# Attention of a macaron block: maxima split out of PSUM, keys projected on four column strips, numerators of two heads in one PSUM bank

## The chip, the cores and the metric

The kernel runs on one core of a Trainium2 chip. The metric is the device time of one execution in microseconds, lower is better. A core has five engines that run their own instruction streams in order: TensorE (PE in the profile, its weight loads PEld), VectorE (DVE), ScalarE (ACT), GpSimd (POOL) and SyncE (SP), which issues most transfers; 16 DMA engines move the data.

## The reference

The input x is 16 sequences (batches) of 512 tokens with 128 features, float32. Six steps follow each other, each added to x:

```python
x = x + 0.5 * _L0_ffn_ref(_layernorm(x), ...)   # small per-channel network ("kan")
x = x + _L0_attn_ref(_layernorm(x), ...)        # causal attention
x = x + 0.5 * _L0_ffn_ref(_layernorm(x), ...)
x = x + 0.5 * _L1_ffn_ref(_layernorm(x), ...)   # 8 experts choose 128 tokens each
x = x + _L1_attn_ref(_layernorm(x), ...)        # linear recurrence over tokens
x = x + 0.5 * _L1_ffn_ref(_layernorm(x), ...)
```

The change lies in the causal attention. It has 16 query heads of 8 features in 4 groups; the 4 heads of a group share one key and one value head. Queries and keys are turned by rotary cosines and sines:

```python
q = (x @ Wq) ...; k = (x @ Wk) ...; v = (x @ Wv) ...
q = q * cos + rotate_half(q) * sin
k = k * cos + rotate_half(k) * sin
att = softmax(where(causal, q @ k.T * HD ** -0.5, lowest))
y = (att @ v) @ Wo
```

## The kernel before

Sizes: P = 128 partitions, S = 512 tokens in NT = 4 chunks of 128, HD = 8, NR = 4 groups of NG = 4 heads.

**Queries and keys** (`attn_in`, L414 to L485). After the norm, xT holds a batch transposed, features on partitions. Queries are projected to [128, 512] (`ps_pa`, and with swapped halves `ps_pb`), keys and their swapped form in one matmul to [64, 512] (`ps_pk`, L435), values to `ps_v` (L443). DVE multiplies them by cosines and sines out of PSUM, POOL adds (L439, L462). `parts` (L392) splits a float32 value into three bfloat16 parts: a cast on ACT and three subtractions on POOL. `spread` writes the parts to DRAM (`qs`, `ks`), and transfers bring them back into the packed tiles: a group's `qp[r]` has 72 rows, every pair of query part and key part by 8 features; `kp` has the matching rows. So one bfloat16 matmul over 72 rows gives a score of float32 precision. Rows 96 to 98 of `qp` get the negated row maximum in three parts, against rows of ones in `kp`.

**Maxima** (`maxima`, L596). For batch b+1, scores with queries on partitions go to `ps_sc`, one tile per entry of `BANKS` (11 per group), and DVE reduces each to row maxima (L615, L620) in `maxs`, 32 columns per half of the heads. `max_rows` (L624) splits them into three bfloat16 parts with four operations on [128, 32], transposes each chunk on PE (`ps_m`, L641), copies the result to `mr` [24, 512] and sends it over DRAM (`ms`) into rows 96 to 98 of two `qp` tiles.

**Weights and numerators** (`weights`, L656; `outputs`, L684). For batch b, scores with keys on partitions and the maximum already subtracted go to `ps_st`; ACT takes the exponential into `pt`, POOL clears what lies above the diagonal (L678). Per group, 16 matmuls (`ps_av`, L696) multiply by the values `va`, 32 columns wide per head: 8 values, a column of ones (the denominator), the rest zeros. The 4 heads of a group lie on the four strips of 32 partitions of one bank. ACT copies the bank to `oT`, PE transposes it (`ps_oq`, L709), DVE divides (L713, L714) into `y`. `stage_out` multiplies by Wo and goes on.

**Order.** The order of PE, ACT, DVE and POOL is written out by hand by generators. A loop over batches (L1144) has 44 turns, one score tile of `weights` and one of `maxima` each; the other stages (`kan`, `attn_in`, `outputs`, `gated`) are generators in `urgent` and `sides` that emit a piece per turn. `need` and `take` (L220, L226) give each turn a budget per engine, `bank` hands out two PSUM banks (tag `mm`), `later` holds work for the start of the next turn. `taken` counts groups whose weights are emitted; `attn_in` waits on it before it overwrites a `qp` tile. Before the loop there is a fill (b = -1, `filling`): the first batches' `kan` and `attn_in`, and the maxima of batch 0 alone. After the loop the experts run (`experts`, L896), with the recurrence between their two rounds.

**Queues.** SP issues nearly all transfers in program order: loads, `qs`, `ks`, `kp`, `qp`, `ms`. ACT's queue issues eight small loads at the start.

## Time and profile before

| | us |
|---|---|
| three runs | 1643.77, 1643.75, 1638.86 |
| median | 1643.75 |
| profiled execution | 1642.42 |
| its span | 1640.6 |
| PE busy in the span | 1542.4 (94%) |
| DVE, ACT, POOL busy | 1134.6, 1007.3, 1020.0 |
| share of PE in the chain that ended last | 70%; DVE 18% |

The span runs from the first to the last instruction. Matmuls are pipelined, so busy PE is not PE at its peak, and a row's mean duration is longer than what one more matmul adds. A row such as `L709 PE MATMUL ps_oq<-ident,oT 128*128 128x128 f32 x256 | 39.4, 276 | 0.5` reads: source line, engine, operation, result from operands, shape, count; busy us and mean ns; idle time of the engine just before, and what ended it. The chain is followed back from the last instruction, at each step to what released it or to the instruction before it on its engine.

### The profile page before, as it was taken

The numbers are of one execution on the slowest core, as the hardware profiler recorded it, in microseconds if no ns is written. First come the engines' busy times: TensorE is split into PE (matmuls) and PEld (weight loads), VectorE is DVE, ScalarE is ACT, GpSimd is POOL, SyncE is SP. The second block draws the span as 40 slices with busy tenths as digits, with TensorE's granted clock in tenths as the row PEclk, the third lists the DMA queues.
The fourth block names the chain that finished last, engine by engine and source line by source line (L and its number), as shares of the span: only waits on it lengthen the run. The fifth ranks groups of instructions, "written<-read, shape, count | busy, mean of one in ns | idle before, by whom it ended". The sixth has DMA issues, their size and how long they took to land.

```text
span 1640.6 us, 35158 instructions
## 1 busy us (share of the span) xinstructions
PE 1542.4 (94%) x12813; PEld 1074.8 (66%) x12813; DVE 1134.6 (69%) x3616; ACT 1007.3 (61%) x2016; POOL 1020.0 (62%) x1486
## 2 busy tenths in 40 slices
PE   5689999999999999999998899999999999999998
PEld 2234444444445444445454479999998899999998
DVE  6577878888888888888988334875569654762322
ACT  3336667877778777777766866444453444545444
POOL 2634555566655664565553666767766677777774
PEclk9779989999999999999999999999999999999999
DMA  5210110111111100110122213333332333333333
GB/s 128 66 66 24 54 50 28 41 57 50 31 43 52 56 26 36 57 43 29 45 71 62 58 41 62 69 66 73 69 73 56 72 62 78 70 71 73 74 73 57
DMA packets 103252, 94.91 MB, mean 58 GB/s; under 512 B 13229, under 2 KB 91638, under 8 KB 102838
## 3 DMA queue, kind: packets, MB, share of 16 engines
q1 hardware_dynamic: 76220, 67.72, 13.3%
q0 software_dynamic: 26048, 24.93, 9.0%
q8 instruction: 101, 1.65, 0.4%
q14 instruction: 73, 0.60, 0.1%
q10 hardware_dynamic: 810, 0.02, 0.0%
HBM read 59.07 MB, written 37.49 MB: 59 GB/s over the span
## 4 chain that ended last, share of the span: by engine, by line
PE 70%; DVE 18%; ACT 4%; issue 3%; POOL 3%; DMA 1%; SPq 0%; ACTq 0%; DVEq 0%; POOLq 0%
PE ps_h L939 12%; PE ps_y L954 12%; PE ps_av L696 7%; PE ps_st L673 6%; PE ps_sc L610 6%; DVE below L615 5%; PE acc L972 5%; PE ps_kg L364 4%; PE ps_s L337 3%; PE ps_t L317 3%; ACT pt L676 2%; DVE ln_st L286 2%; DVE tok L797 2%; PE ps_ko L385 2%; PE ps_g L749 1%
## 5 line engine op out<-in xcount | busy, mean ns | idle before, releaser
L678 POOL TENSOR_SCALAR_AFFINE_SELECT pt<-pt 128x128 f32<-128x128 f32 (+2 forms) x704 | 250.8, 363 | 333.3 <-ACT pt L676 328.5
L676 ACT ACTIVATE pt<-ps_st 128x512 f32<-128x512 f32 x682 | 368.2, 563 | 96.8 <-PE ps_st L673 91.0
L615 DVE CUSTOM_DVE_ANT_0 below<-ps_sc,causal 128x512 bf16<-128x512 f32 (+1 forms) x512 | 315.1, 615 | 79.9 <-PE ps_sc L610 64.4
L864 POOL DMA_INDIRECT xg<-xnd,tokI x256 | 250.6, 979 | 77.0 <-issue 39.5
L941 ACT ACTIVATE mo<-ps_h 128x512 f32<-128x512 f32 x256 | 152.6, 596 | 232.9 <-PE ps_h L939 232.5
L939 PE MATMUL ps_h<-xin,mw 128*128 128x128 f32 x2048 | 277.6, 278 | 0.0
L954 PE MATMUL ps_y<-mw,mo 128*128 128x128 f32 x2048 | 271.1, 275 | 2.2 <-DVE mo L963 2.2
L610 PE MATMUL ps_sc<-kp,qp 72*128 72x512 bf16 (+3 forms) x1024 | 261.3, 307 | 11.4 <-DVE maxs L615 6.9
L673 PE MATMUL ps_st<-qp,kp 99*128 99x512 bf16 x992 | 251.9, 305 | 16.7 <-ACT pt L676 16.1
L939 PEld LDWEIGHTS ps_h<-xin,mw 128*128 128x128 f32 x2048 | 249.7, 192 | 5.5 <-issue 3.4
L954 PEld LDWEIGHTS ps_y<-mw,mo 128*128 128x128 f32 x2048 | 249.2, 192 | 3.3 <-DVE mo L963 3.1
L986 POOL DMA_INDIRECT sum<-ye,tokI x124 | 201.6, 1626 | 67.5 <-issue 31.8
L673 PEld LDWEIGHTS <-kp 99*128 99x128 bf16 x1024 | 95.2, 101 | 177.8 <-issue 159.9
L370 ACT ACTIVATE kan_h<-kan_s,rbias,kw 128x512 f32<-128x512 f32 x256 | 205.7, 812 | 3.5 <-PE ps_kg L364 3.5
L696 PE MATMUL ps_av<-pt,va 128*32 128x512 f32 (+3 forms) x2048 | 164.4, 439 | 0.0
L620 DVE TENSOR_REDUCE maxs<-ps_sc 128x2 f32<-128x512 f32 (+1 forms) x192 | 130.1, 685 | 39.1 <-PE ps_sc L610 38.7
L610 PEld LDWEIGHTS <-qp 72*128 72x128 bf16 x1024 | 97.1, 100 | 80.1 <-issue 57.5
L960 DVE TENSOR_TENSOR mo<-mo 128x128 bf16<-128x128 f32 x132 | 38.2, 289 | 129.4 <-ACT mo L945 129.2
L972 PE MATMUL acc<-mo 128*128 128x128 bf16 x1584 | 111.4, 219 | 3.9 <-DVE mo L960 3.8
L696 PEld LDWEIGHTS ps_av<-pt,va 128*32 128x32 f32 x2048 | 53.5, 109 | 93.6 <-issue 43.0
L972 PEld LDWEIGHTS <-mo 128*128 128x128 bf16 x1584 | 99.4, 98 | 18.8 <-issue 17.6
L293 POOL TENSOR_TENSOR ln_rstd<-ln_rstd,mhalf 128x4 f32<-128x4 f32 x96 | 100.5, 1047 | 8.0
(194 smaller groups left out, 2340.5 us busy)
## 6 DMA issues: line engine op xcount, KB each, us to landing
qp<-qs SPq DMA_DIRECT2D x64, 288.0 KB
xnd<-kan_x SPq DMA_DIRECT2D x32, 256.0 KB
sum<-x SPq DMA_DIRECT2D x31, 256.0 KB
qs<-qpart SPq DMA_DIRECT2D x48, 128.0 KB
kp<-ks SPq DMA_DIRECT2D x48, 96.0 KB
x<-in_L_attn_x_dram SPq DMA_DIRECT2D x16, 256.0 KB
mw<-in_L_ffn_w_dram SPq DMA_DIRECT2D x16, 256.0 KB
xg<-xnd,tokI POOLq DMA_INDIRECT x256
```

The costliest lines, as they stand in the source:

```text
L370: nc.scalar.activation(h, sk[half], AF.Relu, bias=rbias[:, half, v : v + 1], scale=kw1[:, half, v : v + 1])
L610: nc.tensor.matmul(v[:, u, 0:n], lhsT=qp[r][0 : 9 * HD, g, bass.ts(c, P)], rhs=kp[0 : 9 * HD, r, 0:n], start=alone, stop=(u == len(gs) - 1 ...
L615: nc.vector.tensor_tensor_reduce(below[:, 0:n], v[:, 0, 0:n], causal[:, S - n : S], 1.0, LOWEST, ALU.add, ALU.max, accum_out=maxs[:, c, h ...
L673: nc.tensor.matmul(v[:, u, 0:n], lhsT=kp[ROWS, r, bass.ts(c, P)], rhs=qp[r][ROWS, g, c * P : S], start=True, stop=True)
L676: nc.scalar.activation(o, v[:, :, 0:n], AF.Exp, scale=HD ** -0.5)
L678: nc.gpsimd.affine_select(out=dg, in_=dg, compare_op=ALU.is_ge, fill=0.0, base=0, pattern=[[0, len(gs)], [1, P]], channel_multiplier=-1)
L696: nc.tensor.matmul(po[32 * g : 32 * g + 32, c * P : S], lhsT=va[:, c, r, :], rhs=pt[:, g, OFF[c] : OFF[c] + n], start=(c == 0), stop=(c == ...
L864: nc.gpsimd.indirect_dma_start(out=xgs[i // E % 2][:, i % E, :], out_offset=None, in_=xnd[b], in_offset=bass.IndirectOffsetOnAxis(ap=tokI[ ...
L939: nc.tensor.matmul(pst[:, f, :], lhsT=mw1[e][:, bass.ts(f, P)], rhs=xins[i // E % 2][:, i % E, :], start=True, stop=True)
L954: nc.tensor.matmul(py, lhsT=hs[u][:, f, :], rhs=mw2[e][:, f, :], start=(f == 0), stop=(f == NF - 1))
L972: nc.tensor.matmul(acc[:, c, :], lhsT=sels[u][:, bass.ts(c, P)], rhs=yes[u][:, w, :], start=(e == 0 and c == 0 and w == 0), stop=(e == las ...
L986: nc.gpsimd.indirect_dma_start(out=sums[k, b], out_offset=bass.IndirectOffsetOnAxis(ap=tokI[g][:, n : n + 1], axis=0), in_=ye[:, b % 2 * ( ...
```

## The change

- **Keys.** Keys are projected chunk by chunk: 8 matmuls of 128 columns put each chunk of 128 tokens on its own strip of 32 partitions, so that the keys are [128, 128] instead of [32, 512], plain and swapped side by side in one bank, the values behind them in the same bank. One product with a new table `ropek` (8 small loads on ACT's queue) replaces two; the addition, cast and subtractions run on 128 columns. The feature order of `wk` is changed.
- **Packed rows.** The rows of `qp` and `kp` stand in another order: in `qp` the three copies of a row are neighbours, in `kp` the three parts. Each `kp` transfer reads all three parts; a wait on `taken` stands before them.
- **Maxima.** They are written into one of two fixed tiles `topped` [128, 128], cleared once; one float32 transpose puts 32 of its columns on partitions, and four operations split them there, reading PSUM. `ms` is written in runs of 128 tokens, in the fill from ACT's queue.
- **Numerators.** Of two groups, the second's values stand 16 columns further in `va`, and both accumulate into one bank; copy, transposes and division happen once for two groups. The rows of `wo` are loaded in the matching order, in 8 transfers behind the loads of x.
- `parts` takes POOL's budget as an argument, 0.5 for keys; `stage_out` waits two turns more in the loop.

```diff
...
         nc.scalar.dma_start(out=gate_sb, in_=gate_in)
+        KR = NR * HD
+        ropek = cst.tile([P, 2, P], F32, name="ropek")
+        for j in range(NT):
+            for w in range(2):
+                src = rope_in[0:HD, w, bass.ts(j, P)].unsqueeze(1).to_broadcast([HD, NR, P])
+                nc.scalar.dma_start(out=ropek[j * KR : (j + 1) * KR, w, :], in_=src)
         rbias = cst.tile([P, 2, NV], F32, name="rbias")
...
         w2d = cst.tile([P, 2, NV, MH], F32, name="w2d")
+        topped = [cst.tile([P, P], F32, name=f"topped{i}") for i in range(2)]
+        for i in range(2):
+            nc.gpsimd.memset(topped[i], 0.0)
         eye4 = cst.tile([P, MH], F32, name="eye4")
...
-        KR = NR * HD
         wq = cst.tile([D, NH, HD], F32, name="wq")
         nc.sync.dma_start(out=wq, in_=wq_in.rearrange("k (h d) -> k h d", d=HD))
-        wk = cst.tile([D, 2, NR, HD], F32, name="wk")
-        nc.sync.dma_start(out=wk[:, 0, :, :], in_=wk_in.rearrange("k (h d) -> k h d", d=HD))
+        wk = cst.tile([D, 2, HD, NR], F32, name="wk")
+        nc.sync.dma_start(out=wk[:, 0, :, :].rearrange("k d h -> k (d h)"), in_=wk_in)
         wv = cst.tile([D, KR], F32, name="wv")
...
         wo = cst.tile([D, D], F32, name="wo")
-        nc.sync.dma_start(out=wo, in_=wo_in)
         rope = cst.tile([P, 2, S], F32, name="rope")
...
             load(b)
+        for i in range(NR // 2):
+            for g in range(NG):
+                src = wo_in[i * M : (i + 1) * M, :].rearrange("(j g d) n -> g j d n", j=2, g=NG)[g]
+                nc.sync.dma_start(out=wo[i * M + g * 2 * HD : i * M + (g + 1) * 2 * HD, :], in_=src)
         hh = HD // 2
...
+        def spread_keys(part, name):
+
+            scr = tc.dram_tile([3, HD, NR, S], BF16, name=name)
+            for i in range(3):
+                nc.sync.dma_start(out=scr[i].rearrange("d r (j t) -> j (d r) t", j=NT), in_=part[:, i, :])
+            return scr
+
         def attn_in(b, st):
             _, xT = yield from norm(x[b])
-            ka = w1p.tile([KR, S], F32, name="rope_ka")
-            kb = w1p.tile([KR, S], F32, name="rope_kb")
+            ka = w1p.tile([P, 2, P], F32, name="rope_ka")
             ta = w1p.tile([P, S], F32, name="rope_a")
...
             qpart = w1p.tile([P, 3, S], BF16, name="qpart")
-            kpart = w1p.tile([KR, 3, S], BF16, name="kpart")
+            kpart = w1p.tile([P, 3, P], BF16, name="kpart")
             pa = yield from bank([P, S], F32, "ps_pa", 0.9)
...
             freed()
-            pk = yield from bank([2 * KR, S], F32, "ps_pk", 0.9)
-            nc.tensor.matmul(pk, lhsT=wk.rearrange("k w h d -> k (w h d)"), rhs=xT, start=True, stop=True)
-            later.append(lambda: nc.vector.tensor_mul(ka, pk[0:KR, :], rope[0:KR, 0, :]))
+            pkv = yield from bank([P, 3, P], F32, "ps_kv", 1.3)
+            for w in range(2):
+                for j in range(NT):
+                    nc.tensor.matmul(pkv[j * KR : (j + 1) * KR, w, :], lhsT=wk[:, w, :, :].rearrange("k d h -> k (d h)"),
+                                     rhs=xT[:, bass.ts(j, P)], start=True, stop=True)
+            pv = pkv[:, 2, :].rearrange("p (c n) -> p c n", n=KR)
+            for c in range(NT):
+                nc.tensor.matmul(pv[:, c, :], lhsT=xT[:, bass.ts(c, P)], rhs=wv, start=True, stop=True)
+            later.append(lambda: nc.vector.tensor_mul(ka, pkv[:, 0:2, :], ropek))
             yield
...
             nc.gpsimd.tensor_tensor(ta, ta, tb, ALU.add)
-            take(dve=0.7)
-            pv = yield from bank([P, NT, KR], F32, "ps_v", 0.9)
-            for c in range(NT):
-                nc.tensor.matmul(pv[:, c, :], lhsT=xT[:, bass.ts(c, P)], rhs=wv, start=True, stop=True)
-            later.append(lambda: nc.vector.tensor_mul(kb, pk[KR : 2 * KR, :], rope[KR : 2 * KR, 1, :]))
-            yield
-            take(dve=0.7)
-            freed()
-            qp_steps = parts(ta, qpart, nc.scalar.copy, act=0.6)
+            take(dve=0.4)
+            qp_steps = parts(ta, qpart, nc.scalar.copy, 1.15, act=0.6)
             step(qp_steps)
...
             va = vap.tile([P, NT, NR, 32], F32, name="va")
-            nc.gpsimd.memset(va[:, :, :, HD:32], 0.0)
-            nc.gpsimd.memset(va[:, :, :, HD : HD + 1], 1.0)
-            later.append(lambda: nc.vector.tensor_copy(va[:, :, :, 0:HD], pv.rearrange("p c (r d) -> p c r d", d=HD)))
-            yield
-            take(dve=0.3)
+            nc.gpsimd.memset(va, 0.0)
+            mine = [va[:, :, j::2, 2 * HD * j : 2 * HD * (j + 1)] for j in range(2)]
+            for to in mine:
+                nc.gpsimd.memset(to[:, :, :, HD : HD + 1], 1.0)
+
+            def values():
+                from_ = pv.rearrange("p c (r j d) -> p c r j d", j=2, d=HD)
+                for j, to in enumerate(mine):
+                    nc.vector.tensor_copy(to[:, :, :, 0:HD], from_[:, :, :, j, :])
+
+            later.append(values)
+            yield
+            take(dve=0.4)
             freed()
...
             def keys():
-                yield from need(pool=1.25)
-                nc.gpsimd.tensor_tensor(ka, ka, kb, ALU.add)
-                yield
-                yield
-                yield
-                yield from parts(ka, kpart, nc.scalar.copy, act=0.6)
+                yield from need(pool=0.5)
+                keys_ = ka[:, 0, :]
+                nc.gpsimd.tensor_tensor(keys_, keys_, ka[:, 1, :], ALU.add)
+                yield
+                yield
+                yield from parts(keys_, kpart, nc.scalar.copy, 0.5, act=0.3)
...
-            ks = spread(kpart, NR, f"ks{b}")
+            ks = spread_keys(kpart, f"ks{b}")
             qs = spread(qpart, NH, f"qs{b}")
             N = 3 * HD
-            for j in range(3):
-                nc.sync.dma_start(
-                    out=kp[j * N : (j + 1) * N, :, :],
-                    in_=ks[j].rearrange("d r t -> d (r t)").unsqueeze(0).to_broadcast([3, HD, NR * S]),
-                )
+            while taken[0] < NR * (b - NKP + 1):
+                yield
+            for i in range(3):
+                nc.sync.dma_start(out=kp[i * N : (i + 1) * N, :, :],
+                                  in_=ks.rearrange("j d r t -> d j (r t)"))
             for r in range(NR):
...
                 nc.sync.dma_start(out=qp[r][0 : 3 * N, :, :],
-                                  in_=src.unsqueeze(0).to_broadcast([3, N, NG * S]))
-            yield
-
-        def centered(ps, w):
+                                  in_=src.unsqueeze(1).to_broadcast([N, 3, NG * S]))
+            yield
+
+        def centered(ps, w, to=None):
...
             nc.tensor.matmul(ps, lhsT=center, rhs=w, start=True, stop=True)
-            nc.vector.tensor_copy(w, ps)
+            if to is None:
+                nc.vector.tensor_copy(w, ps)
+            else:
+                nc.vector.tensor_copy(to, ps.rearrange("k (h d) -> k d h", d=HD))
...
             for half in range(2):
-                maxs = w2p.tile([P, NT, NH // 2], F32, name="maxs")
+                maxs = topped[half][:, 0 : NT * NH // 2].rearrange("p (h c) -> p h c", c=NT)
                 for r in (2 * half, 2 * half + 1):
...
                                 below[:, 0:n], v[:, 0, 0:n], causal[:, S - n : S], 1.0, LOWEST,
-                                ALU.add, ALU.max, accum_out=maxs[:, c, h : h + 1],
+                                ALU.add, ALU.max, accum_out=maxs[:, h, c : c + 1],
                             )
                         else:
-                            nc.vector.tensor_reduce(maxs[:, c, h : h + len(gs)], v[:, :, 0:n], AX.X, ALU.max)
+                            nc.vector.tensor_reduce(maxs[:, h : h + len(gs), c], v[:, :, 0:n], AX.X, ALU.max)
                         yield
-                urgent.append(max_rows(b, half, maxs))
-
-        def max_rows(b, half, maxs):
+                urgent.append(max_rows(b, half))
+
+        def max_rows(b, half):
             H2 = NH // 2
+            N = NT * H2
+            yield
+            pm = yield from bank([P, P], F32, "ps_m", 0.2)
+            nc.tensor.transpose(pm, topped[half], ident)
+            r = pm[0:N, :]
+            mr = w1p.tile([N, 3, P], BF16, name="mr")
+
+            def first():
+                nc.vector.tensor_scalar_mul(mr[:, 0, :], r, -1.0)
+                nc.vector.scalar_tensor_tensor(mr[:, 1, :], in0=r, scalar=-1.0, in1=mr[:, 0, :],
+                                               op0=ALU.mult, op1=ALU.subtract)
+
+            later.append(first)
+            yield
+            take(dve=0.45)
             yield from need(dve=0.45)
-            ms = w2p.tile([P, NT, 3, H2], BF16, name="ms")
-            r = w2p.tile([P, NT, H2], F32, name="ms_r")
-            nc.vector.tensor_scalar_mul(ms[:, :, 0, :], maxs, -1.0)
-            nc.vector.scalar_tensor_tensor(r, in0=maxs, scalar=-1.0, in1=ms[:, :, 0, :],
-                                           op0=ALU.mult, op1=ALU.subtract)
-            yield
-            yield from need(dve=0.45)
-            nc.vector.tensor_copy(ms[:, :, 1, :], r)
-            nc.vector.tensor_sub(ms[:, :, 2, :], r, ms[:, :, 1, :])
-            yield
-            yield
-            pm = yield from bank([3 * H2, NT, P], BF16, "ps_m", 0.3)
-            for c in range(NT):
-                nc.tensor.transpose(pm[:, c, :], ms[:, c, :, :].rearrange("p i h -> p (i h)"), identb)
-            mr = w1p.tile([3 * H2, S], BF16, name="mr")
-            later.append(lambda: nc.vector.tensor_copy(mr, pm.rearrange("p c q -> p (c q)")))
-            yield
-            take(dve=0.4)
-            freed()
+            nc.vector.scalar_tensor_tensor(r, in0=r, scalar=-1.0, in1=mr[:, 0, :], op0=ALU.mult, op1=ALU.subtract)
+            nc.vector.tensor_sub(mr[:, 2, :], r, mr[:, 1, :])
+            freed()
+            yield
             scr = tc.dram_tile([3, H2, S], BF16, name=f"ms{b}_{half}")
-            nc.sync.dma_start(out=scr.rearrange("i h t -> (i h) t"), in_=mr)
+            queue = nc.scalar if filling[0] else nc.sync
+            queue.dma_start(out=scr.rearrange("i h (c t) -> (h c) i t", c=NT), in_=mr)
             for k in range(2):
-                nc.sync.dma_start(out=packed(b)[0][2 * half + k][MXR : MXR + 3, :, :],
+                queue.dma_start(out=packed(b)[0][2 * half + k][MXR : MXR + 3, :, :],
                                   in_=scr[:, k * NG : (k + 1) * NG, :])
...
             pt, va, y = st["pt"].pop(r), st["va"], st["y"]
-            yield
-            po = avp.tile([P, S], F32, name="ps_av")
+            pair, odd = r // 2, r % 2
+            yield
+            if not odd:
+                st["po"] = avp.tile([P, S], F32, name="ps_av")
+            po = st["po"]
             for c in range(NT):
...
                     nc.tensor.matmul(po[32 * g : 32 * g + 32, c * P : S], lhsT=va[:, c, r, :],
-                                     rhs=pt[:, g, OFF[c] : OFF[c] + n], start=(c == 0), stop=(c == NT - 1))
+                                     rhs=pt[:, g, OFF[c] : OFF[c] + n], start=(c == 0 and not odd),
+                                     stop=(c == NT - 1 and odd == 1), skip_group_check=True)
                 if c == NT - 1:
                     st["read"] = r + 1
-                    oT = w2p.tile([P, NT, P], F32, name="oT")
-                    later.append(lambda: nc.scalar.copy(oT.rearrange("p c q -> p (c q)"), po))
+                    if odd:
+                        oT = w2p.tile([P, NT, P], F32, name="oT")
+                        later.append(lambda: nc.scalar.copy(oT.rearrange("p c q -> p (c q)"), po))
                 if c in (0, NT - 1):
                     yield
+            if not odd:
+                return
             take(act=0.6)
...
             yield
-            pq = yield from bank([P, NT, NG, 32], F32, "ps_oq", 0.5)
+            pq = yield from bank([P, NT, 2 * NG, 2 * HD], F32, "ps_oq", 0.5)
             for c in range(NT):
                 nc.tensor.transpose(pq[:, c, :, :].rearrange("p r w -> p (r w)"), oT[:, c, :], ident)
-            rd = small.tile([P, NT, NG, 1], F32, name="rden")
+            rd = small.tile([P, NT, 2 * NG, 1], F32, name="rden")
...
                 nc.vector.reciprocal(rd, pq[:, :, :, HD : HD + 1])
-                nc.vector.tensor_mul(y[:, :, r, :, :], pq[:, :, :, 0:HD], rd.to_broadcast([P, NT, NG, HD]))
+                nc.vector.tensor_mul(y[:, :, pair, :, :], pq[:, :, :, 0:HD],
+                                     rd.to_broadcast([P, NT, 2 * NG, HD]))
...
             freed()
-            st["out"].append(r)
+            st["out"].extend((r - 1, r))
             yield
...
             while len(st["out"]) < NR:
+                yield
+            if not hurry[0]:
+                yield
                 yield
...
             if b >= 0:
-                sts[b]["y"] = w2p.tile([P, NT, NR, NG, HD], F32, name="y")
+                sts[b]["y"] = w2p.tile([P, NT, NR // 2, 2 * NG, HD], F32, name="y")
                 sts[b]["out"] = []
...
```

## The prediction

> **What bounds the kernel now.** I read the page first, then the busy times by stretch, the groups by line and shape, the chain that ended last, and the SP queue in order of time. The stretches, cut where the first score matmul of the weights starts (117) and where the experts fill TensorE (960), are (length, busy time and instructions of PE, PEld, DVE, ACT, POOL, then clock, DMA share, GB/s):
>
> ```profile
> 0.00:117.00 117.00, 78.12 (x284) 33.71 (x285) 76.11 (x211) 43.71 (x65) 48.35 (x67) 0.82 0.32 91
> 117.00:927.00 810.00, 767.13 (x5857) 389.76 (x5855) 676.02 (x2156) 602.43 (x1109) 460.85 (x935) 0.98 0.14 46
> 927.00:960.00 33.00, 28.99 (x223) 13.82 (x220) 7.09 (x25) 26.42 (x51) 27.46 (x51) 1.00 0.10 29
> 960.00:1641.00 681.00, 668.12 (x6458) 637.48 (x6456) 375.39 (x1224) 334.74 (x792) 483.31 (x435) 1.00 0.32 68
> ```
>
> The reader is to see four stages: a fill of 117 us with no full engine; the attention loop, 16 batches in 810 us (50.6 each), PE busy 95% of it and DVE 83%; a hand-over of 33 us led by ACT and POOL; 681 us of experts, 98% PE. The change touches nothing that the last stage runs, so I cost it at nothing there; the loop decides. Its rows that the change touches, and rows that give new prices (form, count, total us, mean ns, idle before):
>
> ```profile
> L709 PE MATMUL ps_oq<-ident,oT 128*128 128x128 f32 x256 | 39.4, 276 | 0.5
> L641 PE MATMUL ps_m<-identb,ms 128*24 128x128 bf16 x128 | 12.8, 224 | 4.3 <-DVE ms L636 4.3
> L435 PE MATMUL ps_pk<-kan_xT,wk 128*64 128x512 f32 x32 | 17.2, 618 | 1.9 <-DVE rope_a L424 1.9
> L696 PE MATMUL ps_av<-pt,va 128*32 128x128 f32 x512 | 25.7, 273 | 0.0
> L729 PE MATMUL ps_o<-wo,yT 128*128 128x128 f32 x128 | 16.9, 274 | 0.0
> L701 ACT COPY oT<-ps_av 128x512 f32<-128x512 f32 x64 | 37.4, 584 | 44.7 <-PE ps_av L696 44.7
> L462 POOL TENSOR_TENSOR rope_ka<-rope_ka,rope_kb 32x512 f32<-32x512 f32 x16 | 20.1, 1258 | 0.0
> L631 DVE SCALAR_TENSOR_TENSOR ms_r<-maxs,ms 128x32 f32<-128x32 f32 x32 | 14.2, 444 | 1.1
> ```
>
> Matmuls are pipelined, so a total divided by its count is the time one adds: 154 ns for a numerator transpose, 100 ns for a maxima transpose, 50 ns for a 128-column pass on a 32-column strip (four strips run beside each other), 132 ns for such a pass over the whole array. A float32 matmul is two passes.
>
> **The change in the loop, part by part.**
>
> PE. Numerators: 256 transposes become 128, -39.4/2 = -19.7. Maxima: 128 bfloat16 transposes become 32 float32 ones at 154 ns, 12.8 to 4.9 = -7.9. Keys: one 512-column matmul per batch becomes 8 of 128 columns, 8 x 2 x 16 = 256 passes; at 50 ns 12.8, so -4.4; if the strips did not overlap, at 132 ns 33.8, so +16.6. I take 50 ns, because L696 has the same 32-column form and also changes its moving operand from strip to strip. Values keep their 128 passes. Sum -32.0, with the other end of the strips -11.0. Accumulating the second head into the bank adds no instruction.
>
> DVE. Keys: two products of 32x512 from PSUM (676 and 682 ns) become one of 128x256; a copy of that form from PSUM (L890) takes 414 ns: 16 x (1.358-0.42) = -15.0. Splitting the maxima: rows L630, L631, L635, L636, L643 are 251+444+227+408+406 = 1.74 us per half; now four operations of 32x128, which I price by the 128x128 PSUM forms L714 (291) and L963 (341): 1.26 us, 32 x -0.48 = -15.4. Division: 64 x (242+291) becomes 32 x (353, the 128x32 reciprocal L776, + 414) = -9.6. Values: two copies at 210 instead of one at 282, +2.2. Sum -38.
>
> ACT: 32 copies of 584 ns go, -18.7; 16 key casts fall from 606 to about 291 ns (L945, 128x128), -5.0. POOL: four key operations per batch (1258, 1176, 1151, 1145 ns) shrink from 512 to 128 columns; between 233 ns (L292, 4 columns) and about 1180 a straight line gives 0.46 us (bounds 0.32, the 128x128 select of L678, and 0.6): 75.6 to 29, -46; clearing all of va and writing ones twice adds 16 x 0.25 = +4.
>
> What of this lies on the path? I added up the pieces of the chain that ended last between 120 and 920 us: PE 552, DVE 166, ACT 51, issue 28, POOL 8. It looks like this around a batch's keys (start, us, piece):
>
> ```profile
> 322.26 1.02 PE ps_pk L435 x2
> 323.28 0.03 issue
> 323.30 0.68 DVE rope_ka L436
> 323.98 0.60 DVE below L615
> 324.59 0.10 DVE ms L630
> 324.69 0.02 issue
> 324.72 1.23 DVE ms_r L631
> ```
>
> On the chain the touched pieces are ps_oq 12.5, ps_m 6.2, ps_pk 13.1, rope_ka and rope_kb 10.2, the maxima split 11.9, reciprocal and y 8.3, va 1.9, oT 4.1. Scaled by the ratios above they give 6.3 + 3.8 + 3.4 + 7.1 + 3.3 + 2.3 - 0.9 + 2.1 + 0.9 for POOL's key pieces = 28.3. The pure PE count gives 32.0. Since all four engines lose 24 to 42 us, no parallel chain is left standing in the way; I take **-28**.
>
> In that chain L631 took 1.23 us at 324.72, against its mean of 444 ns, and ended with POOL's rope_a add, which ran 1.28 us from 324.61. The Trainium skill (SBUF — State Buffer, SBUF: two separate sides) says that VectorE with two SBUF inputs and GpSimd take one port pair in turn, the loser blocking fully. By that rule the new split, with at most one SBUF input each, is not blocked, and the sum stays -28; if the stretching had another cause and stayed, the split would give nothing on the chain (1.86 us against 1.74 per half, +0.8 for -3.3) and the sum would be -24. The row prices, taken from PSUM forms, go with the first.
>
> **New waits and moved steps.** The transpose of the maxima now stands two turns after the last maximum instead of four. PE is in order, so it waits if VectorE is late, and behind it stand the next turn's score matmuls, hence exponentials and maxima. At the chain's 322 us the last reduction ends at 322.99, and PE would reach the transpose after the second pair of score matmuls, at 324.9: no wait. Bounds: 0 (less 4.3, the present wait in row L641, if that goes), and 0.69 (reduction) + 0.69 (a product queued before it) = 1.38 us, 32 times. I take 0, with 1.9 us of room at that place. The bank is held for two turns longer, while one fewer bank is taken for keys and two fewer per batch for numerators: nothing. The new wait for the old keys (taken at 4(n-2) for batch n) is the one that the second queries' slot has already; it delays the issue of kp by at most a quarter batch, 13 us of the cover below.
>
> Packed rows: the transfers out of qs and ks now run over 3 engines of 16, as this microsecond between 109 and 110 shows, DMA share 0.20 at 82 GB/s:
>
> ```profile
> 109.00:110.00 1.00, 1.00 (x3) 0.46 (x2) 0.86 (x3) 0.00 (x0) 0.00 (x0) 0.50 0.20 82
> ```
>
> and the SP queue in order of time (start, length of the issue):
>
> ```profile
> 103.71 0.47 SPq L648 DMA_DIRECT2D ms<-mr  x1
> 114.18 0.56 SPq L650 DMA_DIRECT2D qp<-ms  x2
> ```
>
> The issue at 114.18 waits for ms to land: 10.5 us, because it lay behind qp and kp on those engines. With 24 outermost rows instead of 3 copies the transfer may take a third of 288 KB / 80 GB/s = 3.7 us. In the loop I cost both forms at nothing: batch 4's last keys are issued at 227 and first read at 269, 42 us of cover; if it went, it would be PE's first maxima of a batch that wait. Keys and maxima now leave in 256-byte runs (before, 1 KB). Against this speaks the Trainium skill (DMA: Bandwidth & Descriptors, Specifications): line rate needs 512 bytes. By it those writes may double; the sum stays, with 13 us between the first kp issue and its reader, and no run here shows the price.
>
> **Fill, start, hand-over.** Start: ACT's queue gets 8 more issues, at 0.27 to 0.87 us (its present ones), say 0.6: 4.8. ACT is ready at 7.5 and first needed at 11.8, 4.3 of cover: +0.5 (0 to 2.7). Moving wo behind the loads and into 8 issues costs SP about 4 us after 25, where it idles until 44; wo is read after 200. Fill: batch 0's PE waits through ACT's key cast, which waits for POOL: -0.8 - 0.3 = -1.1. Batch 1's norm waits until 71.8 for POOL to finish three key operations: 3 x -0.75 = -2.3. Batch 2's keys and one split on DVE: -1.0. ms on ACT's queue makes ACT wait for a round trip (1.4 us for the second half, 123.56 to 124.95); ACT idles 9.6 us there, nothing. Hand-over: one oT copy less on the chain, -0.6. The two extra turns of the output stage and the later emission leave all stages within ten turns of their place: nothing.
>
> Sum: 1642.4 (the profiled execution: span 1640.6 + 1.8 around it) - 28 + 0.5 - 4.4 - 0.6 = **1610**. That execution lies 1.3 under the median shown (1643.75), 3.6 over the lowest.
>
> **Rivals.** (1) The strips do not overlap: +21 on PE, 1610 + 21 = 1631. Against it, row L696. (2) Slower: PE waits at the maxima transpose each time for reduction and product, 1.38 x 32 = 44, 1654. From 1.0 us per half the gain is gone, from 1.15 it shows as slower. For it: in order, two turns less of distance; against it, the room above. (3) The path closes up: DVE, 83% now, sets the pace through its maxima and the loop keeps its length, 1638 to 1649. Against it: DVE loses as many us as PE. (4) More: of the 43 us in which PE stands idle in the loop (810 - 767) half goes too, because POOL and ACT release pt earlier (PE waited 33 us for POOL's pt at L696's weight loads): 1589.
>
> **How the numbers follow.** Forecast 1599 to 1624: 0.62. Rival 1: 0.14. Rival 2: 0.09. Rival 3: 0.05. Rival 4: 0.10. Same means within 0.3%, 5 us, about what can be measured here. Faster 0.62 + 0.14 + 0.10 = 0.86, same 0.05, slower 0.09. The range drops half of rival 4 and rivals 2 and 3 (0.19): 1592 to 1638.
>
> **What will show it.** Right: the loop near 782 us with the experts still 681; ps_oq near 20, ps_m near 5, the strip matmuls near 13 us busy; oT x32; DVE near 1097. A ps_m row with tens of us of idle from a maxs line shows rival 2; strip passes over 100 ns each show rival 1; a first weights matmul later than 113 shows the fill wrong. Wrong altogether if PE's idle time grows by what its work loses.

## The result and the profile after

The changed kernel takes 1647.4 us (median; 1644.3 to 1649.2) against 1640.3 (1636.8 to 1645.4) of the kernel before, each run 20 times on one chip: ratio 1.0039 (95% interval 1.0032 to 1.0047), slower by 6.4 us. The forecast was 1610 us, 1592 to 1638. The profiled execution took 1644.3 us, span 1642.4. Its stages, cut as those of before (windows; columns as there):

```profile
0.00:117.00 117.00, 80.70 (x324) 34.95 (x325) 72.24 (x211) 41.88 (x64) 40.25 (x72) 0.80 0.34 92
117.00:927.00 810.00, 754.58 (x5837) 382.67 (x5835) 641.01 (x2065) 583.25 (x1086) 425.70 (x952) 0.98 0.16 46
927.00:962.00 35.00, 28.75 (x203) 13.37 (x203) 5.91 (x21) 23.46 (x44) 26.71 (x48) 0.90 0.08 24
962.00:1642.40 680.40, 667.91 (x6454) 637.10 (x6452) 376.67 (x1225) 334.71 (x792) 482.79 (x434) 1.00 0.32 68
```

The second stretch is cut at the same places in both kernels, and the loop itself has its old length too: from the first exponential to the end of the last it takes 835.3 us (117.2 to 952.5), before 835.1 (117.6 to 952.6). There is less work in it on every engine: in the 810 us shown, PE went from 767 to 755, DVE from 676 to 641, ACT from 602 to 583, POOL from 461 to 426. The work went, the time stayed. The groups that answer to those shown of before:

```profile
L744 PE MATMUL ps_oq<-ident,oT 128*128 128x128 f32 x128 | 19.3, 273 | 0.1
L657 PE MATMUL ps_m<-ident,topped 128*128 128x128 f32 x32 | 9.3, 290 | 0.0
L454 PE MATMUL ps_kv<-kan_xT,wk 128*32 128x128 f32 x256 | 10.3, 279 | 0.4 <-DVE rope_a L441 0.4
L734 ACT COPY oT<-ps_av 128x512 f32<-128x512 f32 x32 | 18.7, 585 | 28.2 <-PE ps_av L727 28.2
L663 DVE SCALAR_TENSOR_TENSOR mr<-ps_m,mr 32x128 bf16<-32x128 f32 x32 | 8.9, 279 | 1.1
L406 ACT CAST qpart<-rope_a 128x512 bf16<-128x512 f32 x16 | 9.9, 618 | 33.2 <-POOL rope_a L462 33.2
L476 DVE COPY va<-ps_kv 128x64 f32<-128x64 f32 x32 | 5.7, 219 | 23.1 <-POOL va L468 23.1
```

Rows one, three, four and five are close to the forecast prices or below them; the second, ps_m, was forecast at 4.9 us. The last two show, in their third column, two waits that the prediction does not have. Here is one place where both happen (order of time; start, length, engine, work, idle time before):

```profile
486.59 1.27 POOL L462 TENSOR_TENSOR rope_a<-rope_a,rope_b 128x512 f32<-128x512 f32 x1
...
487.80 0.52 POOL L468 MEMSET va<- 128x512 f32 x1
487.89 0.62 ACT L406 CAST qpart<-rope_a 128x512 bf16<-128x512 f32 x1 [1.97 <-POOL rope_a L462]
488.36 0.35 DVE L476 COPY va<-ps_kv 128x64 f32<-128x64 f32 x2 [1.90 <-POOL va L468]
...
488.63 0.68 DVE L642 CUSTOM_DVE_ANT_0 below<-ps_sc,causal 128x512 bf16<-128x512 f32 x1
...
489.06 0.38 PE L701 MATMUL ps_st<-qp,kp 99*128 99x512 bf16 x1 [0.25 <-ACT pt L704]
```

POOL is in order: its addition waits behind a mask, its clearing of va behind the addition. ACT's cast stands waiting for the addition, and the exponentials stand behind it; DVE's value copies wait for the clearing, and the maxima stand behind them. The change had brought all of this into one turn: the bank of the values, and with it a turn between the addition and what needs it, was gone, and va was now cleared whole, the values' own columns too.

The decisive view is the loop by batches. Cut at every 44th exponential of the weights (one per turn), batches 3, 4, 5, 6, 10 and 11 of the changed kernel are:

```profile
270.09:321.79 51.70, 47.68 (x363) 24.18 (x358) 39.34 (x132) 36.68 (x70) 25.56 (x60) 0.98 0.13 41
321.79:379.19 57.40, 52.82 (x408) 26.29 (x407) 42.16 (x138) 42.10 (x79) 31.21 (x67) 1.00 0.14 42
379.19:436.76 57.57, 54.63 (x437) 28.07 (x436) 42.94 (x140) 42.65 (x80) 31.49 (x68) 1.00 0.14 42
436.76:488.42 51.66, 50.27 (x406) 26.05 (x405) 42.25 (x137) 40.78 (x78) 29.58 (x67) 1.00 0.16 46
644.45:695.51 51.06, 47.80 (x371) 24.00 (x371) 44.61 (x149) 39.34 (x74) 29.29 (x63) 1.00 0.17 47
695.51:758.08 62.57, 56.95 (x438) 28.53 (x438) 50.14 (x159) 42.26 (x79) 33.18 (x71) 0.97 0.14 39
```

and batch 5 of the kernel before, where 3 to 8 are all alike:

```profile
377.57:431.45 53.88, 51.56 (x401) 26.22 (x399) 45.42 (x143) 42.26 (x77) 33.04 (x64) 1.00 0.14 45
```

An ordinary batch fell from 53.9 to 51.7 us, 2.2 less, more than the 1.75 (28/16) of the forecast. But batches 4 and 5 take 3.5 to 3.7 us more than before and batch 11 takes 7.0 more. The matmul counts show that work has moved between batches: in before every batch up to 12 holds the preparation (`attn_in`) of one later batch; now batches 3 and 10 hold none (x363, x371), and 5 and 11 hold parts of two (x437, x438). The counts alone do not explain the lengths: a batch without a preparation is not shorter (51.7, 51.1), and batch 4 (x408) has about the matmuls of batch 6 (x406) but takes 57.4 us instead of 51.7. Batches 4, 5 and 11 are 6 to 11 us longer than an ordinary one. Where a preparation falls can be told by the turn in which POOL adds rope_a: in before turns 0 to 3 of a batch from batch 3 on, in the changed kernel turn 39 of batch 2, 6 of 4, 6 and 43 of 5, 43 of 6 to 8, 0 of 10, 5 and 43 of 11. The hand-written planner books each piece in a turn's budget, so a removed turn and smaller bookings move everything that follows. The last batch is longer too, 41.5 us instead of 39.0; it is 41 to 42 us in every kernel here that has the pairs of numerators and 38 to 40 in those without, and its granted clock is lower with the pairs (0.92 here, 1.00 before).

### The profile page after: what moved, and what is told of

It reads as the page before. It is cut to its first block, busy times and chain, and to the rows that moved or that the text cites. A ratio compares the mean times of both kernels' runs of the same rounds, so it can differ in the third digit from the quotient of the medians.

```text
span 1642.4 us, 35032 instructions
## 1 busy us (share of the span) xinstructions
PE 1531.9 (93%) x12813; PEld 1068.1 (65%) x12813; DVE 1095.8 (67%) x3520; ACT 983.3 (60%) x1984; POOL 975.4 (59%) x1504
## 4 chain that ended last, share of the span: by engine, by line
PE 69%; DVE 19%; ACT 6%; POOL 3%; issue 2%; DMA 1%; ACTq 0%; SPq 0%; DVEq 0%; POOLq 0%
PE ps_h L978 12%; PE ps_y L993 12%; PE ps_av L727 8%; PE ps_st L701 6%; PE ps_sc L637 6%; PE acc L1011 5%; DVE below L642 4%; PE ps_kg L375 4%; PE ps_s L348 3%; ACT pt L704 3%; DVE topped L647 3%; PE ps_t L328 2%; DVE ln_st L297 2%; ACT kan_h L381 2%; DVE tok L836 2%
## 5 line engine op out<-in xcount | busy, mean ns | idle before, releaser
L727 PE MATMUL ps_av<-pt,va 128*32 128x512 f32 (+3 forms) x2048 | 167.7, 445 | 0.0
L647 DVE TENSOR_REDUCE topped<-ps_sc 128x2 f32<-128x512 f32 (+1 forms) x192 | 129.6, 683 | 16.6 <-PE ps_sc L637 15.8
L727 PEld LDWEIGHTS ps_av<-pt,va 128*32 128x32 f32 x2048 | 53.6, 109 | 93.9 <-issue 45.1
```

Source lines behind the costliest of these rows:

```text
L727: nc.tensor.matmul(po[32 * g : 32 * g + 32, c * P : S], lhsT=va[:, c, r, :], rhs=pt[:, g, OFF[c] : OFF[c] + n], start=(c == 0 and not odd) ...
```

## The experiments

The expectations say image for batch. Lengths below are of batches 3 to 8, 10 and 11 in the profiled run; "turn" is that of POOL's addition in these batches, read from the order of time. POOL can run late, so 43 and 0 can be the same place of the plan: e4 and e6 have one plan and read 0 and 43, and e5, with the plan of the changed kernel, reads 7, 6 and 0 where that reads 6, 6 and 43. All times are medians, all ratios are to the kernel before, measured beside each kernel on the same chip.

| kernel | us | ratio (95%) | turn | batches 3, 4, 5, 6, 7, 8 | 10, 11 |
|---|---|---|---|---|---|
| before | 1640 | 1 | 0 | 53.9 53.9 53.9 54.0 53.9 53.9 | 58.5 55.6 |
| changed | 1647.4 | 1.0039 (1.0032-1.0047) | 6, 43 | 51.7 57.4 57.6 51.7 51.7 51.7 | 51.1 62.6 |
| e1_va_apart | 1640.5 | 1.0001 (0.9989-1.0012) | as changed | 51.9 61.6 59.5 51.7 50.7 50.7 | 50.9 60.3 |
| e2_ropek_sp | 1644.5 | 1.0029 (1.0015-1.0042) | as changed | 51.7 57.4 57.6 51.7 51.7 51.7 | 51.1 62.6 |
| e3_both | 1639.9 | 0.9988 (0.9978-0.9998) | as changed | 51.9 61.5 59.5 51.7 50.7 50.7 | 50.9 60.3 |
| b1_wait_only | 1639.8 | 0.9994 (0.9983-1.0006) | as before | 53.9 in each | 58.5 55.6 |
| e5_late_copy_same_plan | 1634.0 | 0.9958 (0.9942-0.9975) | as changed | 51.8 59.2 56.8 51.2 50.3 50.3 | 50.6 59.0 |
| e6_early_copy_other_plan | 1613.2 | 0.9828 (0.9807-0.9850) | 43 | 50.2 or 50.3 in each | 54.5 55.5 |
| e4_copy_later | 1604.3 | 0.9756 (0.9733-0.9780) | 0 | 49.8 or 49.9 in each | 52.2 53.7 |
| e7_change_copy_later | 1619.0 | 0.9870 (0.9849-0.9891) | 0 | 51.7 or 51.8 in each | 55.8 53.5 |

**The two waits on POOL, first round.** e1 clears only what DVE does not write, e2 moves the loads of ropek, e3 does both, b1 puts the wait into the kernel before.

```diff
 # e1, e3
-            nc.gpsimd.memset(va, 0.0)
+            nc.gpsimd.memset(va[:, :, 0::2, HD:32], 0.0)
+            nc.gpsimd.memset(va[:, :, 1::2, 0 : 2 * HD], 0.0)
+            nc.gpsimd.memset(va[:, :, 1::2, 3 * HD : 32], 0.0)
 # e2, e3: the loop over ropek's loads stands behind that of rope
-                nc.scalar.dma_start(out=ropek[j * KR : (j + 1) * KR, w, :], in_=src)
+                nc.sync.dma_start(out=ropek[j * KR : (j + 1) * KR, w, :], in_=src)
 # b1, in the kernel before
-            nc.gpsimd.memset(va[:, :, :, HD:32], 0.0)
+            nc.gpsimd.memset(va, 0.0)
```

> The changed kernel, but POOL zeroes of va only the columns that DVE does not write (three clearings in place of one), so that DVE's two value copies wait for nothing on POOL. Theory A (the wait): in the changed kernel DVE stood 23.1 us in 15 waits for POOL's clearing of va, each with the maxima queued behind it, and this ate most of the gain that PE's shorter work should have given; without it the time falls by about 23 us, to 1618-1632 us, and the row of the value copies waiting for POOL is gone. Rival B (the pace): what PE was relieved of goes into idle time anyway, because its score banks wait for DVE's maxima and ACT's exponentials in every turn; then the row goes, the waits of PE for the maxima and of ACT for the scores stay, and the time stays within 5 us of 1647. Rival C (the clock): the lower granted clock in the loop (nine stretches at half speed against four) is what costs; then the time moves only as far as the number of those stretches does.

> The changed kernel with the eight loads of ropek on SP's queue behind the rope table in place of ACT's queue ahead of its table load. Theory (the start): ACT's table load moves back from 12.8 to about 6.2 us and its first copy from 14.1 to about 11.8 us, so the whole rest of the kernel starts 2.3 us earlier: 1644-1646 us. Rival: the fill absorbs it (the first weights matmul stood at 116.5 us, against 116.9 in the kernel before, though its start was 2.3 us later): no change, within 1 us of 1647.

> Both edits on the changed kernel: va's clearing apart from the value copies, and ropek's loads on SP's queue. Theory A and the start add up: 1616-1630 us, faster than the kernel before by 10 us or more. Rival B (the pace): 1640-1647 us. Rival C (the clock): as far as the half-speed stretches in the loop go from nine back to four, 5-8 us: about 1640 us.

> The kernel before with one edit: POOL clears the whole of va (512 columns a partition) where it cleared 384, so DVE's value copy has to wait for it, as in the changed kernel. In this kernel the clearing stands a turn earlier than the copy (in the trace of before at 159.53-160.1 us), so the wait may be short. Theory A: the wait is dear wherever POOL is late; if POOL's clearing ends after the copy's turn as in the changed kernel (up to 1.9 us an image), slower by 5-20 us. Rival: POOL is on time here, the wait is there but empty and the time stays within 2 us of 1640; then it is the place of the clearing in the changed kernel, right behind the addition of rope_a, that makes the wait long.

Neither theory A nor rival B as written. e1 took the wait of the value copies away altogether and gained some 6 us of the 23: one microsecond in batches 7 and 8, nothing in 6, and the long batches stayed long. In e2 ACT started as it did before (first copy at 11.80 us, in the changed kernel 14.10), but the time cannot be told from the changed kernel's, nor could e3's from e1's. The median lies inside the theory's range, but the first exponential stands at 117.8 us, in the changed kernel at 117.2: the earlier start does not reach the loop. In b1 the wait is nearly empty (1.1 us in 3), since there a turn lies between clearing and copy, and costs nothing. e3's 1639.9 is theory C's figure, but not by its condition: e1 and e3 still have nine stretches at half clock in the loop. C falls as the cause: batches 4 and 5 of the changed kernel were long at a granted clock of 1.00. But the clock adds to the time: e3's batch 4 took 61.5 at 0.92, and the loop of the changed kernel has 46 us at half clock, that of before 28. The profiled executions of b1 and before differ by 17 us of half clock (11 and 28) and by 4.3 us of time; by this one pair, as an estimate, the 17 us more of half clock in the changed kernel are worth about 4 us.

**A turn later.** The other wait, of ACT's cast for the addition, can be made shorter by giving the turn back:

```diff
 # e4 (on e3), e7 (on the changed kernel), e8 (on p_keys_only)
             qp_steps = parts(ta, qpart, nc.scalar.copy, 1.15, act=0.6)
-            step(qp_steps)
```

> e3_both with ACT's copy of the queries' first part (qpart) issued one turn after POOL's addition that it needs, as in the kernel before, where a whole turn lay between them; the changed kernel had taken that turn out together with the bank of the values, and ACT stood 23.3 us in 13 waits there, its exponentials queued behind it. Theory A2 (a second wait): the waits of qpart for rope_a fall below 6 us, the idle time of PE ahead of ps_st falls back towards 15 us, and the time falls by 6-15 us against e3_both (1639.9), to 1625-1634 us. Rival B (the pace: the turns in which PE was relieved are set by DVE and ACT anyway, and the clock gate takes the rest): the wait goes and the time stays within 3 us of e3_both.

1604.3 us, 36 less than e3, a better time than either branch: far more than the 23 us that ACT had waited there in the loop, of which 12 were left. The planner's bookings had moved with it: the addition now runs at turn 0 of every batch from 3 on, and batches 3 to 8 are all alike. e5 and e6 part the two. e5 keeps e3's plan and writes the cast out one turn later; e6 has e4's plan with the cast right behind the addition.

```diff
 # e5, on e3
-            qp_steps = parts(ta, qpart, nc.scalar.copy, 1.15, act=0.6)
+            qp_steps = parts(ta, qpart, lambda *to: copies.append(to), 1.15, act=0.6)
...
         def turn():
             flush()
+            for to in copies:
+                nc.scalar.copy(*to)
+            copies.clear()
 # e6, on e4
+            nc.scalar.copy(qpart[:, 0, :], ta)
-            qp_steps = parts(ta, qpart, nc.scalar.copy, 1.15, act=0.6)
+            qp_steps = parts(ta, qpart, lambda *to: None, 1.15, act=0.6)
```

> e3_both with the plan of turns as it was (which turn takes which piece of side work), but ACT's copy of the queries' first part written out one turn later, behind that turn's exponential. e4_copy_later did two things at once: it took the copy away from POOL's addition, and it moved pieces between turns (the preparation of images 5, 6, 7, 12 and 13 starts at other turns, and images 4, 5 and 11 of the loop, which took 60, 58 and 60 us in e3_both, take 50, 50 and 54 us). If the wait alone was dear: 1603-1612 us, the three images at 50-54 us. If the plan alone: 1636-1642 us. If both: in between, with the regular images near 50 us and the three long ones still long, some 1620-1628 us.

> The other corner: e4_copy_later's plan of turns, but ACT's copy written out right behind POOL's addition, as in the changed kernel. If the wait alone is dear: near e3_both, 1634-1642 us, qpart waiting over 20 us for rope_a. If the plan alone: 1602-1610 us. If both: 1615-1628 us, regular images near 52 us and no image over 56.

> The changed kernel with only the copy a turn later (va cleared whole, ropek on ACT's queue as in the change). The wait of the value copies for va's clearing and the start come back: 6-8 us over e4_copy_later, 1609-1613 us. If the value copies' wait is hidden once ACT runs free: within 3 us of e4, 1603-1607 us.

The four corners are 1639.9 (e3), 1634.0 (cast later), 1613.2 (other plan), 1604.3 (both). Batch 4 of e3 and of e6 (windows):

```profile
319.20:380.74 61.54, 57.22 (x407) 27.67 (x406) 42.51 (x137) 42.24 (x79) 30.30 (x69) 0.92 0.14 39
311.81:362.06 50.25, 49.38 (x402) 26.04 (x398) 41.65 (x139) 40.07 (x77) 29.01 (x68) 1.00 0.17 48
```

e5 fell between its second branch and its third, e6 between its second and its third. The plan is worth 27 to 30 us, the cast's wait 6 to 9. Some of the plan's share comes by way of the clock: the loop has 51 us at half clock in e3 and 34 in e6, 38 in e5 and 31 in e4, which at the price of b1 and before is an estimated 2 to 4 us. e6 still waits 34.3 us for rope_a over the whole run, and its batches 3 to 8 are only 0.4 us longer than e4's. e7 against e4 prices the other wait where the plan is good: e7 missed both branches, at 14.7 us over e4. DVE waits 25.2 us in 15, 1.7 each; batches 3 to 8 are 1.9 us longer each, the other ten together little. So in an ordinary batch the va wait costs its full length in e4's plan, and 1.0 us or nothing in the changed kernel's (e1). The ordinary batches of e7 are as long as those of the changed kernel, 51.7 us: the 28 us between these two kernels lie in the other batches. Batches 4, 5 and 6 of e7 and of e4 (windows):

```profile
310.80:362.54 51.74, 49.79 (x399) 25.96 (x398) 42.45 (x137) 40.42 (x75) 29.63 (x66) 1.00 0.16 46
362.54:414.30 51.76, 49.80 (x399) 25.95 (x398) 42.47 (x137) 40.42 (x76) 29.63 (x66) 1.00 0.17 46
414.30:466.04 51.74, 49.79 (x399) 25.96 (x398) 42.45 (x137) 40.41 (x75) 29.63 (x66) 1.00 0.16 46
```

```profile
312.10:361.89 49.79, 49.17 (x399) 26.00 (x398) 41.55 (x137) 40.19 (x75) 29.50 (x68) 1.00 0.17 48
361.89:411.69 49.80, 49.18 (x399) 26.00 (x398) 41.56 (x137) 40.20 (x75) 29.51 (x68) 1.00 0.18 48
411.69:461.50 49.81, 49.19 (x399) 26.00 (x398) 41.58 (x137) 40.20 (x76) 29.52 (x68) 1.00 0.17 48
```

In e4 PE is busy 49.2 of 49.8 us: this is the loop that the prediction had in mind.

**Evenness or place?** The constant IN says from which turn of a batch a next batch may be started. Changing it moves the plan and leaves every instruction in place.

```diff
-IN, OUT = 38, 8
+IN, OUT = 42, 8      # r1, on the changed kernel; 34, 8 in r3 (changed kernel) and r4 (e4)
...
+            yield                                            # r2, on e4
             yield from together(qp_steps, keys())
```

> The changed kernel, every instruction and wait as it is, with the next image's preparation allowed to start at turn 42 of an image in place of 38. The additions then stand at turns 252, 296, 340 and so on in steps of 44, where the changed kernel has 241, 296, 340, 377: two preparations in one image, none in another. If the plan cost some 27 us (e6 against e3): 1615-1625 us, no loop image between 4 and 8 over 54 us, while the waits of va (20 us or more) and of qpart (20 us or more) stay. If the waits were the cause: 1640-1650 us.

> e4_copy_later with one more turn ahead of the steps on queries and keys, so that ACT's copy stands two turns behind POOL's addition. The rest of the wait (12.4 us in 11) goes; the additions stand at 253, 297, 341 in steps of 44. At 0.45 us an image, as the first turn was worth between e6 and e4: 1596-1602 us. If the rest of the wait is hidden: 1602-1608 us.

> The changed kernel with the preparation allowed to start at turn 34 in place of 38; nothing else. POOL's addition of rope_a then stands at turn 40 of an image for images 5 to 11 (42, 0 and 41 for 12 to 14), where the changed kernel has 40, 7, 7, 0, 0, 0, 0, 1, 6, 0. If the place in the image is the cause, and turn 7 the dear one: no image of the loop between 3 and 8 over 53 us, 1618-1632 us (ratio 0.987-0.995). If any move of the plan costs or gains at random: the images at 53-56 us and the ratio 1.00 or more.

> e4_copy_later with the preparation allowed to start at turn 34: its addition stands at turns 40 and 42 in turn, where e4 has it at turn 0 in every image from 4 on (49.8 us each). If turns 40-42 are as good as turn 0: ratio 0.970-0.980, as e4. If turn 0 is the better place: 0.980-0.990.

| kernel | us, and before measured beside it | ratio (95%) | turn | batches 3, 4, 5, 6, 7, 8 | 10, 11 |
|---|---|---|---|---|---|
| r1_start_42 | 1691.0, 1664.2 | 1.0163 (1.0140-1.0186) | 6 | 54.9 in each | 59.2 57.7 |
| r3_start_34 | 1662.9, 1640.1 | 1.0136 (1.0116-1.0156) | 39 | 55.5 55.5 55.9 55.5 55.5 56.1 | 54.9 57.6 |
| r2_two_turns | 1686.0, 1664.2 | 1.0134 (1.0102-1.0165) | 6 | 56.4 54.9 55.0 57.6 54.6 54.6 | 57.9 59.5 |
| r4_late_34 | 1618.0, 1640.1 | 0.9860 (0.9841-0.9879) | 39, 41 | 51.5 52.2 51.5 52.2 51.5 52.2 | 53.6 52.0 |

Batch 5 of r1 and batch 4 of r3 (windows):

```profile
386.04:440.92 54.88, 51.49 (x400) 26.11 (x399) 41.19 (x139) 40.33 (x77) 29.76 (x66) 1.00 0.14 44
330.04:385.51 55.47, 51.75 (x396) 26.64 (x398) 42.26 (x135) 40.49 (x76) 29.90 (x66) 0.98 0.14 43
```

r1 and r2 missed on every branch; r3 and r4 came out at their second one. r1 and r3 have one preparation in every batch and are slower than the uneven plan that they replaced, so evenness is not what counts. What does is where the stages stand to each other: with the same instructions an ordinary batch takes 51.7 us with the addition at turn 43 (at 0 in e7, where the cast comes later), 54.9 with it at turn 6, 55.5 at turn 39; on e4's code 49.8, then 54.6 to 57.6 (with one turn more), and 51.5 to 52.2. The constant moves the preparation and the small network ahead of it together, and which meeting with the other generators is the dear one stays open; it was not tried.

**The parts alone**, each on the kernel before. In p_pairs_only the reciprocals' tile comes from a pool of two.

> The kernel before with the pairs of numerators alone (two heads' numerators in one bank, va's columns in two places, Wo's rows reordered, half the copies, transposes and divisions; the reciprocals' tile taken from a pool of two). PE loses 18.7 us of transposes in the loop and ACT half of its copies (24 us over the loop). If PE's work sets the loop everywhere: 1620-1625 us. If the turns close up on DVE and ACT (rival B): 1632-1640 us.

> The kernel before with the maxima's split alone (one f32 transpose of the maxima, split from PSUM, ms on ACT's queue in the fill). PE loses 3.7 us in the loop, DVE 4 us (1.11 us in place of 1.23 per half, 32 halves). If PE's work sets the loop: 1634-1637 us; a split that stands later than it did and holds a bank of PSUM longer would show as 1641-1646 us.

> The kernel before with the keys' part alone: keys on four strips with the values in one bank, one transfer for the packed keys, packed rows in the other order, ropek's loads. PE loses 4.2 us, DVE 15 us, POOL 46 us, and one turn an image goes. Theory A2: with that turn POOL's addition and ACT's copy that needs it come into the same turn, ACT waits some 1.8 us an image, and the part loses: 1643-1650 us, with 20 us or more of qpart waiting for rope_a. Rival: POOL's and PE's relief wins: 1632-1638 us.

> p_keys_only with the copy a turn later. It had the same wait (21.6 us in 13) and yet was 15 us faster than the kernel before. If the wait is dear by itself: 1603-1614 us. If it was the arrangement of the turns in the changed kernel that was dear: 1621-1628 us, no gain, since p_keys_only has only one long image (57 us).

| kernel | us | ratio (95%) | batches 3, 4, 5, 6, 7, 8 |
|---|---|---|---|
| p_pairs_only | 1640.6 | 1.0000 (0.9987-1.0014) | 53.1 in each |
| p_max_only | 1633.2 | 0.9955 (0.9938-0.9973) | 50.6 55.4 52.2 52.7 52.7 52.7 |
| p_keys_only | 1625.5 | 0.9908 (0.9891-0.9926) | 54.6 51.6 51.6 51.8 51.6 51.6 |
| e8_keys_copy_later | 1619.3 | 0.9868 (0.9848-0.9887) | 55.3 52.9 52.0 52.0 52.0 52.0 |

p_pairs_only came out at the upper end of rival B, p_max_only a little under its first range, p_keys_only under both of its ranges, e8 between its two. In ordinary batches the parts give 0.8, 1.2 and 2.3 us, 4.2 together, about what e4 has, where the two waits are gone or shorter (53.9 to 49.8, 4.1); the changed kernel has 2.2. As kernels they gain 0, 7 and 15, and the three together lose 6: the ordinary batches add up, the plans do not. p_keys_only waits 21.6 us for rope_a in the loop and is fast all the same; e8 gains on it in the fill and the first two batches, and its ordinary batches are 0.4 us longer.

**Why the keys gain most.** Two kernels give p_keys_only back what it took from POOL and from DVE; what they compute in addition is thrown away.

```diff
 # x_pool_back: the same behind each of the three subtractions of the keys
                 nc.gpsimd.tensor_tensor(keys_, keys_, ka[:, 1, :], ALU.add)
+                nc.gpsimd.tensor_tensor(spare, spare, spare, ALU.add)
 # x_dve_back
             later.append(lambda: nc.vector.tensor_mul(ka, pkv[:, 0:2, :], ropek))
+            later.append(lambda: nc.vector.tensor_mul(spare, pkv[0:KR, :, :].rearrange("p w t -> p (w t)"), rope[0:KR, 0, 0 : 3 * P]))
+            later.append(lambda: nc.vector.tensor_mul(spare[:, 0:P], pkv[0:KR, 0, :], rope[0:KR, 0, 0:P]))
```

> p_keys_only with an addition over 32x384 of a spare tile behind each of POOL's four operations on the keys (its output is thrown away), which gives POOL back some 50 us over the loop; the plan of turns is that of p_keys_only. If POOL's relief carried that part's gain of 15 us (POOL's steps stand in front of the masks that PE's numerators wait for): 1634-1642 us. If it was idle time on POOL: 1625-1628 us.

> p_keys_only with two multiplications from the keys' bank into a spare tile behind the one that is needed (32x384 and 32x128), which gives DVE back 0.85 us an image, some 13 us over the loop. If DVE's relief carried that part's gain: 1634-1640 us. If not: 1625-1629 us.

Ratios 0.9922 (0.9903 to 0.9940) and 0.9972 (0.9958 to 0.9987), against 0.9908 for p_keys_only. Batch 5 of p_keys_only, x_pool_back and x_dve_back:

```profile
377.64:429.23 51.59, 50.37 (x414) 26.58 (x413) 43.05 (x142) 41.27 (x77) 29.72 (x64) 1.00 0.17 47
```

```profile
385.57:437.33 51.76, 50.37 (x414) 26.57 (x413) 43.21 (x142) 41.30 (x77) 32.58 (x68) 1.00 0.16 47
```

```profile
379.88:432.59 52.71, 50.61 (x414) 26.50 (x413) 44.26 (x144) 41.38 (x77) 29.73 (x64) 1.00 0.16 46
```

2.9 us more of POOL cost 0.2 us a batch; 1.2 us more of DVE cost 1.1. Taken as ratios, x_pool_back came out at its second branch and x_dve_back at its first. At these places POOL's relief is nearly worthless, and DVE's counts almost in full.

## Why the prediction was wrong

- **The step that failed** is the last sentence of "Fill, start, hand-over": "The two extra turns of the output stage and the later emission leave all stages within ten turns of their place: nothing." The preparations did stay within ten turns (their additions moved by six at most), and a place six turns on cost 3 us or more a batch (r1, at turn 6, 54.9; the changed kernel's ordinary batches and e7's 51.7). With it fell the sum, which scaled the pieces of the old chain and left everything else where it stood. The plan that the change brought about cost 27 to 30 us against e4's (e3 to e6, e5 to e4), as much as the whole forecast gain; with va cleared whole, as in the change, plan and cast together cost 28 (the changed kernel to e7). Why one place is dear and another not stays open.
- **Waits.** "New waits and moved steps" looked at the transpose of the maxima, where indeed nothing waits (L657, idle 0.0; rival 2 falls), and missed the two others. "Clearing all of va ... adds +4" priced the clearing as POOL's busy time and not what waits for it: about 6 us here, 15 in e4's plan. The cast behind the addition was not priced at all: 6 to 9 us.
- **Prices of work.** Right or cheaper: ps_oq 19.3 (forecast 19.7), DVE in all 1095.8 (1097), oT x32, strips 10.3 (12.8; rival 1 falls), keys on POOL 0.43 to 0.45 us (0.46). Mis-sized: ps_m 9.3 instead of 4.9, because 32 transposes that stand alone took 290 ns each, and 154 was the price in a row of four. On PE the rows named in the forecast lost 30 us, close to its 32, but PE's busy time in the whole run fell by 10.5 (1542.4 to 1531.9): what a row loses is not what the engine loses.
- **The rule on ports.** By the Trainium skill (SBUF — State Buffer, SBUF: two separate sides) VectorE can be blocked by GpSimd when two of its inputs lie in SBUF; the new split has at most one there. The trace agrees: L662, L663, L670 and L671 have means of 271 to 281 ns and none took over 282, though 35 of the 128 ran beside a two-input operation of POOL; L631 had a mean of 444 and a longest of 1225. Two inputs are not the whole condition: of the old split, L630 and L635 read one tile in SBUF and took up to 919 and 1243 ns beside POOL. The maxima alone gained 7.1 us, and the two terms of the chain for it were 3.8 + 3.3. That they meet is partly luck: an ordinary batch of p_max_only gained 1.2 us, 19 over sixteen, and long batches (59.7 instead of 53.2 in batch 12) took the rest back.
- **The chain's shares.** For the keys they gave 3.4 + 7.1 - 0.9 + 0.9 = 10.5; alone they brought 15. For the pairs 6.3 + 2.3 + 2.1 = 10.7; alone they brought 0 (within 2), 0.8 us an ordinary batch. PE's pure count would have been worse: it gives the pairs 19.7 and the keys 4.4.
- **The loop's length.** The prediction read it as 810 us, 50.6 a batch. Its cut at 927 lies inside the last batch of before, which begins at 913.6 and ends at 952.6; sixteen batches took 835 us, and an ordinary one 53.9. The sum does not use this figure.
- **Fill and start.** Forecast -4.4; the first weights matmul stands at 116.5 us instead of 116.9, so the fill's term was about 0, as the text named for this case. ACT's start came 2.3 us later (bounds 0 to 2.7), and e2 shows that this cost nothing measurable.
- **Rivals.** The time fell where rival 3 had it, 1638 to 1649, at 0.05, but not by its mechanism: in ordinary batches the gain was there. "PE's idle time grows by what its work loses" came true over the loop (12.5 us of each), and it came from a few batches.

e4_copy_later, the change with one turn put back, va cleared apart and ropek on SP's queue, is faster than both kernels: 0.9756 (0.9733 to 0.9780).

## What to carry to other kernels

Where a planner writes the order out, a change of work is also a change of plan: cut the loop into its periods, before and after, and compare where each stage starts in the period before multiplying one period's saving. When a turn between a producer and its consumers is removed, list every engine whose next instruction now waits in order for the producer, and what stands behind it. A clearing that covers more than it did can make the writers of the tile wait for it.

## What the runs showed that was not expected

- With the same instructions the batch length moved from 51.7 to 55.5 us by the place of the preparation, and of the network ahead of it, alone; a batch without a preparation was no shorter than one with it.
- DVE operations that read only SBUF are stretched or not by where they fall, those with one operand there too: in x_dve_back the added multiplications account for 0.81 us of batch 5, and the four splitting operations, unchanged in code, grew from 2.5 to 3.4 us. The two runs of their last subtraction took 0.39 us together in p_keys_only and 1.30 there; the two runs of the first, which has one operand, 0.40 and 1.32.
- Measured beside r1, r2 and the x kernels, the kernel before took 1664 us instead of 1640. x_pool_back shows where: its ordinary batches are those of p_keys_only (51.8 and 51.6 us), but from the last exponential to the end it takes 710 us, p_keys_only 689, with the same instructions there. Why is open. The ratios are hardly touched by it, since the time of the kernel before grew by about as much.
